# The column pass of an attention's preparation: columns copied into lines first, the projection in two strips of 64 rows

## The chip, the cores and the metric

The kernel runs on one core of a Trainium2 chip. A core has a matrix engine (TensorE, PE in the profile; its weight loads are listed apart as PEld), a vector engine (VectorE, DVE), a scalar engine (ScalarE, ACT), a general engine (GpSimd, POOL) and a queue engine (SyncE, SP) that here only issues transfers. They share an on-chip memory of 128 partitions (SBUF) and an accumulator memory with as many partitions in eight banks (PSUM), into which TensorE writes.

The metric is the time of one execution on the device in microseconds, the median of several runs. One more execution was recorded by the hardware profiler; its span runs from its first to its last instruction.

## What is computed

The input `x` is float32, (2, 128, 128, 128): two images of 128 channels, 128 rows h and 128 columns w. Four layers follow one another, each as `x = x + layer(group_norm(x))`: an attention along the columns, a recurrent convolution in four directions, a deformable convolution and a convolution in Hadamard form. Only the first is touched. In it every column w of an image is a sequence of 128 positions h:

```python
x = jnp.transpose(x, (0, 3, 1, 2))                 # (n, w, c, h)
x = x.reshape(NW, C, H)                            # 256 sequences
xg = x.reshape(NW, 8, C // 8, H)                   # 8 groups of 16 channels
wg = w_qkv.reshape(8, OUT * 2 // 8, C // 8)        # 32 outputs for each group
qkv = jnp.einsum('bgch,gdc->bgdh', xg, wg).reshape(NW, OUT * 2, H)
qkv = _bn(qkv, g_qkv, b_qkv, (0, 2), (1, OUT * 2, 1))
qkv = qkv.reshape(NW, GROUPS, GP * 2, H)
q, k, v = (qkv[:, :, :GP // 2], qkv[:, :, GP // 2:GP], qkv[:, :, GP:])
qr = jnp.einsum('bgci,cij->bgij', q, q_emb)
kr = jnp.einsum('bgci,cij->bgij', k, k_emb).swapaxes(2, 3)
qk = jnp.einsum('bgci,bgcj->bgij', q, k)
stacked = jnp.concatenate([qk, qr, kr], axis=1)
stacked = _bn(stacked, g_sim, b_sim, (0, 2, 3), (1, GROUPS * 3, 1, 1))
```

The projection `qkv` works within groups: the 32 outputs of a group (8 of q, 8 of k, 16 of v) depend on its own 16 channels alone. The batch norm over `qk` needs the mean and the mean square of all products q·k, and these follow from sums over the positions: for each sequence and group, the products of q with q and of k with k and the plain sums, an 8x8 block each and a column.

## The kernel before

`layer0_prepare` (line 92) keeps both images on chip as `xa[n]`, 128 channels on the partitions and (h, w) behind them, so that a row h is contiguous and the elements of a column lie 128 elements (512 bytes) apart. It has three stages.

The first (lines 116 to 320) loads the images, forms the channels' products for the norms, and folds group norm and batch norm into the projection. For the q and k outputs (k = 0) and the v outputs (k = 1), `psr` spreads scale and shift over all partitions, `rows[:, k]` (line 304, ScalarE) holds them, and `wz[n][:, k, :]` (line 307, VectorE) is the scaled weight matrix: 128 channels by 128 outputs, zero outside the groups' own blocks. Its q and k half has its columns ordered as q of all groups (64), then k of all groups (64).

The second stage is the column pass (lines 361 to 452), which the change is about. It takes 64 turns, each with four columns (`RT`) of one image:

- `sequences(i, vs)` (line 371) projects the four columns. For each column one matmul takes the column of `xa` as its weights (`lhsT`, 128 channels by 128 positions, 512 bytes between neighbours) and streams `wz[n]`, 256 outputs, so that the result has positions on the partitions and outputs along them. Two columns share one PSUM buffer `ps_zb` of one bank; there are four such buffers. VectorE adds the shifts (`along`, line 345) in two additions per pair: the q and k outputs go to `z`, one of two buffers `zb` with a column of ones after every 32 outputs, and the v outputs go to `vs`.
- `moments(z)` (line 400) multiplies the `z` of the turn before: 16 matmuls, each of a block of 32 outputs (four groups' q or k) against itself and the ones, in four column strips of the array. The results land in `ps_m`, where `[:, half, 0]` and `[:, half, 1]` are a q block and the k block of the same groups. ScalarE copies the q part to `gq`, VectorE multiplies it by the k part, GpSimd adds the product to `acc` (line 418).
- After every fourth turn the queue engine stores `vs`, 1 MB, to DRAM (line 432). `vs` has two buffers.

TensorE's order is written out by hand: the projection of turn i, then the moments of turn i - 1. `InOrder` (line 73) fixes this program order on TensorE, VectorE and ScalarE; instructions issued through `nc.vector` or `nc.gpsimd` directly may be moved by the scheduler. After the last turn the sums in `acc` become the scale of `qk` (`logit_scales`, through `psm`) and `onto`.

The third stage (lines 456 to 569) goes over the rows h in the same manner (`positions`, `ps_zt`, `zt`, then `pg`), and its `project` makes the q and k values that attention reads (`ps_q`, `sa`, `sb`). Both use only the q and k half, `wz[n][:, 0, :]`. Attention, `layer0_attention`, comes next; `lg<-qk` in the profile is its product of q and k, with the 8 channels of a group in strips of 32 array rows.

Most instructions are listed under line 81, the helper of `InOrder`, so the profile is read by the names of the tiles.

Of the kernel before, what the change touches and what calls it, by code (L numbers as in the profile page):

```python
# [7 lines left out]
F32 = mybir.dt.float32  # L8
I32 = mybir.dt.int32
AF = mybir.ActivationFunctionType  # L10
ALU = mybir.AluOpType
# [4 lines left out]
P = 128  # L16
N = 2
S = 128
RT = 4
# [72 lines left out]
def layer0_prepare(env, x, prm, mem, alphas):  # L92
# [4 lines left out]

    nc, tc = env.nc, env.tc  # L100
    HW = WC // 2
    with ExitStack() as ctx:
# [6 lines left out]
        strip, ones = late[:, 0:128], late[:, 128:256]  # L109
        gsim = kp.tile([P, NG, 3], F32, name="gsim", tag="gsim")  # L110
        rows = kp.tile([P, 2, 1 + N, P], F32, name="rows", tag="rows")
        wz = [kp.tile([P, 2, P], F32, name=f"wz{n}", tag=f"wz{n}") for n in range(N)]
        shift = kp.tile([P, N], F32, name="shift_qk", tag="shift_qk")
        eg = kp.tile([P, 9, S], F32, name="eg", tag="eg")

        with ExitStack() as early:
# [178 lines left out]
            for k in range(2):  # L295
                psr = pp.tile([P, 1 + N, P], F32, name="psr", tag="psr")
                for s in range(2):
                    dgs = wp.tile([P, 1 + N, P], F32, name="dgs", tag="dgs", bufs=2)
                    for c in range(1 + N):
                        nc.vector.tensor_scalar(  # L300
                            dgs[:, c, :], pick[:, k, s, :], cols[:, s, c : c + 1], None, ALU.mult
                        )
                    nc.tensor.matmul(psr, lhsT=ones, rhs=dgs, start=(s == 0), stop=(s == 1))
                nc.scalar.copy(rows[:, k], psr)
                lo = 256 + 128 * k
                for n in range(N):
                    nc.vector.scalar_tensor_tensor(
                        wz[n][:, k, :],
                        wt[:, lo : lo + P],
                        gs[:, n : n + 1],  # L310
                        rows[:, k, 0, :],
                        ALU.mult,
                        ALU.mult,
                    )
            psq = pp.tile([P, 1 + N], F32, name="psq", tag="ps_small")
            for s in range(2):
                nc.tensor.matmul(
# [27 lines left out]
        def along(n, k, shape):  # L345
            return (
                rows[:, k, 1 + n, :]
                .rearrange("p (b c) -> p b c", b=(4, NG)[k])
                .unsqueeze(1 if k == 0 else 2)
                .to_broadcast(shape)  # L350
            )
# [9 lines left out]
        with ExitStack() as part:  # L361
            sp = part.enter_context(tc.tile_pool(name="l0s", bufs=1))
            gp = part.enter_context(tc.tile_pool(name="l0g", bufs=2))
            pp = part.enter_context(tc.tile_pool(name="l0pm", bufs=2, space=PSUM))
            acc = sp.tile([P, 2, 33], F32, name="acc2", tag="acc2")
            nc.gpsimd.memset(acc, 0.0)
            zb = [sp.tile([P, RT, 4, 33], F32, name=f"zb{j}", tag=f"zb{j}") for j in range(2)]
            for t in zb:
                nc.gpsimd.memset(t[:, :, :, 32:33], 1.0)

            def sequences(i, vs):

                n, w = i // NT, i % NT * RT
                z = zb[i % 2]
                for hf in range(2):
                    ps = pp.tile([P, 2, 2, P], F32, name="ps_zb", tag="ps_zb", bufs=4)
                    for j in range(2):
                        pe.matmul(
                            ps[:, j],
                            lhsT=xa[n][:, :, w + 2 * hf + j],  # L380
                            rhs=wz[n],
                            start=True,
                            stop=True,
                        )
                    dve.tensor_tensor(
                        z[:, 2 * hf : 2 * hf + 2, :, 0:32],
                        ps[:, :, 0, :].rearrange("p w (b c) -> p w b c", b=4),
                        along(n, 0, [P, 2, 4, 32]),
                        ALU.add,
                    )  # L390
                    at = (w + 2 * hf) % HW
                    dve.tensor_tensor(
                        vs[:, :, at : at + 2, :],
                        ps[:, :, 1, :].rearrange("p w (g c) -> p g w c", g=NG),
                        along(n, 1, [P, NG, 2, 16]),
                        ALU.add,
                    )
                return z

            def moments(z):  # L400


                ps = pp.tile([P, 2, 2, 33], F32, name="ps_m", tag="ps_m")
                for half in range(2):
                    for b in range(2):
                        for s in range(4):
                            w, block = 2 * half + s // 2, 2 * b + s % 2
                            pe.matmul(
                                ps[32 * s : 32 * s + 32, half, b, :],
                                lhsT=z[:, w, block, 0:32],  # L410
                                rhs=z[:, w, block, :],
                                start=True,
                                stop=True,
                            )
                gq = gp.tile([P, 2, 33], F32, name="gq", tag="gq")
                act.copy(gq, ps[:, :, 0, :])
                dve.tensor_tensor(gq, gq, ps[:, :, 1, :], ALU.mult)
                nc.gpsimd.tensor_tensor(acc, acc, gq, ALU.add)

            z_last = None  # L420
            for i in range(N * NT + 1):
                if i < N * NT:
                    n, j = i // NT, i % NT
                    if j % 4 == 0:
                        vs = gp.tile([P, NG, HW, 16], F32, name="vs", tag="vs")
                    z = sequences(i, vs)
                if z_last is not None:
                    moments(z_last)
                if i < N * NT:
                    if j % 4 == 3:  # L430
# [25 lines left out]
        with ExitStack() as part:  # L456
# [9 lines left out]
            def positions(t):  # L466

                zs = []
                for n in range(N):
                    z = zt[2 * (t % 2) + n]  # L470
                    ps = pp.tile([P, RT, P], F32, name="ps_zt", tag="ps_zt")
                    for hh in range(RT):
                        pe.matmul(
                            ps[:, hh, :],
                            lhsT=xa[n][:, t * RT + hh, :],
                            rhs=wz[n][:, 0, :],
                            start=True,
                            stop=True,
                        )
                    dve.tensor_tensor(  # L480
                        z[:, :, :, 0:32],
                        ps.rearrange("p h (b c) -> p h b c", b=4),
                        along(n, 0, [P, RT, 4, 32]),
                        ALU.add,
                    )
                    zs.append(z)
                return zs
# [24 lines left out]
            def project(n, wc, b, sa, sb):  # L512
                ps = pp.tile([P, 16, WC], F32, name="ps_q", tag="ps_q")
                pe.matmul(
                    ps,
                    lhsT=wz[n][:, 0, :],
                    rhs=xa[n][:, b * 16 : (b + 1) * 16, wc * WC : (wc + 1) * WC],
                    start=True,
                    stop=True,
# [1631 lines left out]
```

## Time and profile before

| what | value |
|---|---|
| median of 3 runs | 5539.87 us (5536.61 to 5543.36) |
| the profiled execution, own time | 5539.68 us |
| its span | 5537.9 us |
| TensorE busy | 5230.7 us, 94% of the span |
| VectorE, ScalarE, GpSimd busy | 3687.8, 2604.6, 1546.4 us |
| mean granted TensorE clock | 0.973 |
| first projection of the column pass | 110.30 us |
| first projection of the row pass behind it | 271.40 us |

A group line of the profile gives line, engine, operation, output<-inputs, shapes and how often, then busy time and the mean of one in nanoseconds, then the idle time of the engine ahead of the group and what ended it. The groups of the column pass, from the first 500 us of the trace:

```profile
L81 PE MATMUL ps_zb<-wz,xa 128*128 128x256 f32 x512 | 138.1, 414 | 1.0 <-DVE wz L307 1.0
L81 PEld LDWEIGHTS ps_zb<-wz,xa 128*128 128x128 f32 x512 | 118.4, 303 | 5.7 <-DVE wz L307 2.1
L81 DVE TENSOR_TENSOR zb<-ps_zb,rows 128x256 f32<-128x256 f32 x128 | 54.4, 425 | 49.2 <-PE ps_zb L81 41.4
L81 DVE TENSOR_TENSOR vs<-ps_zb,rows 128x256 f32<-128x256 f32 x128 | 53.0, 414 | 0.0
L81 PE MATMUL ps_m<-zb 128*32 128x33 f32 x2048 | 29.5, 198 | 0.0
L81 DVE TENSOR_TENSOR gq<-gq,ps_m 128x66 f32<-128x66 f32 x64 | 14.3, 224 | 0.5 <-ACT gq L81 0.5
L81 ACT COPY gq<-ps_m 128x66 f32<-128x66 f32 x64 | 13.7, 215 | 145.9 <-PE ps_m L81 138.8 <-DVE zb L81 7.1
L418 POOL TENSOR_TENSOR acc<-acc,gq 128x66 f32<-128x66 f32 x64 | 20.8, 325 | 138.4 <-DVE gq L81 138.2
```

Each float32 matmul leaves two records on TensorE and two on its weight loads: 256 columns make 512 records. Matmuls are pipelined, so the mean of one record is longer than the distance between two.

### The profile page before, as it was taken

Reading aid. Unit: us, or ns where it says so; the run is one execution under the profiler, and the core shown is the slowest. Engines: PE = TensorE matmul, PEld = TensorE weight load, DVE = VectorE, ACT = ScalarE, POOL = GpSimd, SP = SyncE. Lnnn points to the kernel's source line nnn. Section 1 sums busy time; section 2 is a strip of 40 time slices with the busy share of each in tenths; the row PEclk is TensorE's granted clock in tenths of the full one; section 3 lists DMA queues with packets and bytes.
Section 4 is the critical chain, followed back from the end, with each engine's and each line's share of the span. In section 5 each row is a group of like instructions: output and inputs, shape, how many; then the busy total and the mean of one; then the engine's idle time right before and its main releaser. Section 6 shows DMA issues by size and latency. Waiting matters only on the chain. (4 is left out here: it accounts for less than half of the span.)

```text
span 5537.9 us, 171854 instructions
## 1 busy us (share of the span) xinstructions
PE 5230.7 (94%) x71931; PEld 4656.8 (84%) x71931; DVE 3687.8 (67%) x7132; ACT 2604.6 (47%) x8118; POOL 1546.4 (28%) x1169
## 2 busy tenths in 40 slices
PE   8997999999999908999999999999899999999999
PEld 6866888888888708999999999994799999999877
DVE  3635888888888866555555556663566666666798
ACT  1056989889888845552223330003233333333322
POOL 2114666666666632000000003330000000000376
PEclk8998999999999959999999999999999999999999
DMA  3353333333333389900000000104677767677111
GB/s 153 108 215 92 61 60 61 62 60 61 60 60 61 68 353 202 105 1 1 1 1 1 1 1 32 47 33 113 112 88 86 88 90 86 89 88 88 42 51 57
DMA packets 673354, 421.01 MB, mean 76 GB/s; under 512 B 325696, under 2 KB 630720, under 8 KB 660672
## 3 DMA queue, kind: packets, MB, share of 16 engines
q1 hardware_dynamic: 667406, 400.69, 39.1%
q8 instruction: 576, 9.44, 0.7%
q10 hardware_dynamic: 5170, 9.23, 0.5%
q14 instruction: 202, 1.65, 0.1%
HBM read 269.09 MB, written 157.45 MB: 77 GB/s over the span
## 5 line engine op out<-in xcount | busy, mean ns | idle before, releaser
L81 PE MATMUL pl<-ln,wl 128*128 128x128 f32 (+1 forms) x10160 | 1240.9, 276 | 9.7 <-DVE ln L81 8.2
L81 PEld LDWEIGHTS pl<-ln,wl 128*128 128x128 f32 x10160 | 1175.8, 190 | 23.0 <-issue 7.1
L81 ACT ACTIVATE e<-e,mx 128x128 f32<-128x128 f32 x2048 | 793.5, 395 | 0.8 <-DVE mx L81 0.8
L81 ACT COPY sm<-ps_s 128x432 f32<-128x432 f32 (+1 forms) x768 | 318.2, 487 | 834.2 <-PE ps_s L81 808.5
L81 POOL TENSOR_TENSOR e<-e,total 128x1024 f32<-128x1024 f32 x256 | 485.6, 1897 | 485.4 <-DVE total L81 473.5
L81 ACT COPY res<-ln 128x64 f32<-128x64 f32 (+1 forms) x1016 | 283.9, 304 | 701.2 <-DVE ln L81 701.2
L81 DVE COPY s<-ps_w 100x1152 f32<-100x1152 f32 x256 | 346.5, 1353 | 334.2 <-PE ps_w L81 334.2
L81 PE MATMUL ps_s<-s,xw 100*128 100x144 f32 x4096 | 546.5, 287 | 8.2 <-DMA xw<-px_d 8.2
L81 POOL TENSOR_TENSOR res<-ln,x1t 128x128 f32<-128x128 f32 x256 | 148.9, 582 | 1429.7 <-DVE ln L81 1429.7
L81 PE MATMUL po<-sm,wdef 128*128 128x256 f32 x2304 | 539.1, 379 | 0.0
L81 PE MATMUL pl<-ln,ws 128*128 128x128 f32 x4064 | 536.8, 273 | 0.0
L81 POOL COPY et<-et 128x1024 f32<-128x1024 f32 x256 | 517.1, 2020 | 33.7 <-DVE et L81 25.5
L81 PEld LDWEIGHTS ps_s<-s,xw 100*128 100x128 f32 x4096 | 518.2, 190 | 9.1 <-DMA xw<-px_d 8.6
L81 DVE TENSOR_TENSOR v<-pl,c 128x128 f32<-128x128 f32 x508 | 148.3, 292 | 539.4 <-PE pl L81 536.2
L81 PEld LDWEIGHTS pl<-ln,ws 128*128 128x128 f32 x4064 | 494.4, 190 | 0.0
L81 ACT ACTIVATE r<-gen,alphas 128x1536 f32<-128x1536 f32 x256 | 394.9, 1542 | 169.2 <-PE gen L81 141.5
L81 PEld LDWEIGHTS po<-sm,wdef 128*128 128x128 f32 x2304 | 419.8, 190 | 47.7
L81 POOL MEMSET col<- 128x10 f32 (+1 forms) x72 | 5.9, 121 | 1461.1 <-DVE res L81 1453.6
L81 ACT ACTIVATION_READ_ACCUMULATOR e<-e,mx 128x1 f32 x2048 | 397.2, 194 | 0.0
L81 DVE SCALAR_TENSOR_TENSOR ln<-v,res 128x128 f32<-128x128 f32 x1016 | 347.2, 342 | 48.6 <-POOL res L81 0.9
L81 PE MATMUL te<-cst_main,e 128*128 128x128 f32 x2048 | 338.4, 288 | 26.6 <-POOL e L81 20.1
L81 DVE COPY et<-te 128x512 f32<-128x512 f32 x512 | 348.4, 681 | 13.4 <-PE te L81 13.0
(244 smaller groups left out, 9144.7 us busy)
## 6 DMA issues: line engine op xcount, KB each, us to landing
xw<-px_d SPq DMA_DIRECT2D x1275, 80.0 KB
xa<-in_x SPq DMA_DIRECT2D x16, 1024.0 KB
v_d<-vs SPq DMA_DIRECT2D x16, 1024.0 KB
qb_d<-sb SPq DMA_DIRECT2D x16, 1024.0 KB
qa_d<-sa SPq DMA_DIRECT2D x8, 2048.0 KB
zz<-qb_d SPq DMA_DIRECT2D x1024, 16.0 KB
vt<-v_d SPq DMA_DIRECT2D x64, 256.0 KB
qk<-qa_d SPq DMA_DIRECT2D x256, 64.0 KB
```

The source lines that it names most:

```text
L81: return lambda *a, **k: self.tc.keep_in_program_order(issue(*a, **k))
```

## The change

- The four columns of a turn are first copied into lines. `columns(i)` lets ScalarE copy them from `xa` to `xc`, where each column is contiguous; `xc` has three buffers, and the copies run two turns ahead.
- The projection becomes two matmuls for each column: channels 0 to 63 (groups 0 to 3) and channels 64 to 127 (groups 4 to 7), each with 64 rows of the array and only the 128 outputs that belong to those groups. Their weights are `wzs[n]`, built by eight small VectorE instructions. `wz[n]` keeps the q and k half for the row pass.
- The result buffer `ps_zb` holds all four columns: two banks, one for each strip, two buffers instead of four. A matmul writes 128 outputs in runs of 16, so that the values of four columns lie side by side.
- VectorE makes three additions for a turn instead of four: two of 256 elements to `z` (q and k), one of 512 to `vs`. The shifts for `z` come from `along_qk`, which GpSimd reorders once.
- The order of blocks in `z` is now per strip, and `moments` picks its blocks accordingly. ScalarE copies all of `ps_m` (132 elements), and GpSimd makes the product that VectorE made, before its sum.

```diff
-        wz = [kp.tile([P, 2, P], F32, name=f"wz{n}", tag=f"wz{n}") for n in range(N)]
+        wz = [kp.tile([P, P], F32, name=f"wz{n}", tag=f"wz{n}") for n in range(N)]
+        wzs = [kp.tile([P, 2, 64], F32, name=f"wzs{n}", tag=f"wzs{n}") for n in range(N)]
+        along_qk = [kp.tile([P, 2, 64], F32, name=f"aqk{n}", tag=f"aqk{n}") for n in range(N)]
...
                 for n in range(N):
-                    nc.vector.scalar_tensor_tensor(
-                        wz[n][:, k, :],
-                        wt[:, lo : lo + P],
-                        gs[:, n : n + 1],
-                        rows[:, k, 0, :],
-                        ALU.mult,
-                        ALU.mult,
-                    )
+                    for s in range(2):
+                        half = slice(64 * s, 64 * s + 64)
+
+                        def own_groups(a):
+                            if k == 1:
+                                return a[half, half]
+                            return a[half].rearrange("p (b s c) -> p b s c", b=2, s=2)[:, :, s]
+
+                        to = wzs[n][half, 1 - k]
+                        nc.vector.scalar_tensor_tensor(
+                            to if k == 1 else to.rearrange("p (b c) -> p b c", b=2),
+                            own_groups(wt[:, lo : lo + P]),
+                            gs[half, n : n + 1],
+                            own_groups(rows[:, k, 0, :]),
+                            ALU.mult,
+                            ALU.mult,
+                        )
+            for n in range(N):
+                nc.vector.scalar_tensor_tensor(
+                    wz[n], wt[:, 256:384], gs[:, n : n + 1], rows[:, 0, 0, :], ALU.mult, ALU.mult
+                )
+                nc.gpsimd.tensor_copy(
+                    along_qk[n].rearrange("p s (b c) -> p s b c", b=2),
+                    rows[:, 0, 1 + n, :].rearrange("p (b s c) -> p s b c", b=2, s=2),
+                )
...
-            def sequences(i, vs):
+            def columns(i):
+
+                n, w = i // NT, i % NT * RT
+                xc = gp.tile([P, RT, S], F32, name="xc", tag="xc", bufs=3)
+                act.copy(xc, xa[n][:, :, w : w + RT].rearrange("p h w -> p w h"))
+                return xc
+
+            def sequences(i, vs, xc):
...
-                for hf in range(2):
-                    ps = pp.tile([P, 2, 2, P], F32, name="ps_zb", tag="ps_zb", bufs=4)
-                    for j in range(2):
+                ps = pp.tile([P, 2, 4, P], F32, name="ps_zb", tag="ps_zb")
+                for j in range(RT):
+                    for s in range(2):
+                        half = slice(64 * s, 64 * s + 64)
                         pe.matmul(
-                            ps[:, j],
-                            lhsT=xa[n][:, :, w + 2 * hf + j],
-                            rhs=wz[n],
+                            ps[:, s].rearrange("p g (k w c) -> p k g w c", k=2, w=RT)[:, :, :, j],
+                            lhsT=xc[half, j, :],
+                            rhs=wzs[n][half].rearrange("p k (g c) -> p k g c", g=4),
                             start=True,
                             stop=True,
                         )
+                def both(k):
+                    return ps[:, :, :, 64 * k : 64 * k + 64].rearrange(
+                        "p s g (w c) -> p (s g) w c", w=RT
+                    )
+
+                for e in range(2):
                     dve.tensor_tensor(
-                        z[:, 2 * hf : 2 * hf + 2, :, 0:32],
-                        ps[:, :, 0, :].rearrange("p w (b c) -> p w b c", b=4),
-                        along(n, 0, [P, 2, 4, 32]),
+                        z[:, :, :, 16 * e : 16 * e + 16].rearrange("p w j c -> p j w c"),
+                        both(1)[:, e::2],
+                        along_qk[n]
+                        .rearrange("p s (j c) -> p (s j) c", j=4)[:, e::2]
+                        .unsqueeze(2)
+                        .to_broadcast([P, 4, RT, 16]),
                         ALU.add,
                     )
-                    at = (w + 2 * hf) % HW
-                    dve.tensor_tensor(
-                        vs[:, :, at : at + 2, :],
-                        ps[:, :, 1, :].rearrange("p w (g c) -> p g w c", g=NG),
-                        along(n, 1, [P, NG, 2, 16]),
-                        ALU.add,
-                    )
+                at = w % HW
+                dve.tensor_tensor(
+                    vs[:, :, at : at + RT, :],
+                    both(0),
+                    rows[:, 1, 1 + n, :]
+                    .rearrange("p (g c) -> p g c", g=NG)
+                    .unsqueeze(2)
+                    .to_broadcast([P, NG, RT, 16]),
+                    ALU.add,
+                )
...
-                            w, block = 2 * half + s // 2, 2 * b + s % 2
+                            w, block = 2 * half + s // 2, 2 * (s % 2) + b
...
-                gq = gp.tile([P, 2, 33], F32, name="gq", tag="gq")
-                act.copy(gq, ps[:, :, 0, :])
-                dve.tensor_tensor(gq, gq, ps[:, :, 1, :], ALU.mult)
-                nc.gpsimd.tensor_tensor(acc, acc, gq, ALU.add)
+                gq = gp.tile([P, 2, 2, 33], F32, name="gq", tag="gq")
+                act.copy(gq, ps)
+                nc.gpsimd.tensor_tensor(gq[:, :, 0, :], gq[:, :, 0, :], gq[:, :, 1, :], ALU.mult)
+                nc.gpsimd.tensor_tensor(acc, acc, gq[:, :, 0, :], ALU.add)
 
             z_last = None
+            xcs = {i: columns(i) for i in range(2)}
             for i in range(N * NT + 1):
+                if i + 2 < N * NT:
+                    xcs[i + 2] = columns(i + 2)
...
-                    z = sequences(i, vs)
+                    z = sequences(i, vs, xcs.pop(i))
```

In the row pass `wz[n][:, 0, :]` becomes `wz[n]`, and the helper `along` is written out where it was used; nothing else changes there.

More of the change, by code (lines that the diff above doesn't have):

```diff
@@ L343, in logit_scales @@
             nc.vector.tensor_tensor(alphas[:, :, to], t3, gsim[:, :, to], ALU.mult)
[L345 to L350, printed above, removed]
-            )
         pe, dve, act = (InOrder(tc, e) for e in (nc.tensor, nc.vector, nc.scalar))
@@ L384, in sequences @@
                         )
-                    dve.tensor_tensor(
-                        z[:, 2 * hf : 2 * hf + 2, :, 0:32],
-                        ps[:, :, 0, :].rearrange("p w (b c) -> p w b c", b=4),
-                        along(n, 0, [P, 2, 4, 32]),
+                def both(k):
[3 more added lines that the diff above has]
+                for e in range(2):
+                    dve.tensor_tensor(
+                        z[:, :, :, 16 * e : 16 * e + 16].rearrange("p w j c -> p j w c"),
[4 more added lines that the diff above has]
+                        .to_broadcast([P, 4, RT, 16]),
                         ALU.add,
                     )
-                    at = (w + 2 * hf) % HW
-                    dve.tensor_tensor(
-                        vs[:, :, at : at + 2, :],
-                        ps[:, :, 1, :].rearrange("p w (g c) -> p g w c", g=NG),
-                        along(n, 1, [P, NG, 2, 16]),
-                        ALU.add,
-                    )
+                at = w % HW
[8 more added lines that the diff above has]
+                )
                 return z
@@ L475, in positions @@
                             lhsT=xa[n][:, t * RT + hh, :],
-                            rhs=wz[n][:, 0, :],
+                            rhs=wz[n],
                             start=True,
@@ L482, in positions @@
                         ps.rearrange("p h (b c) -> p h b c", b=4),
-                        along(n, 0, [P, RT, 4, 32]),
+                        rows[:, 0, 1 + n, :]
+                        .rearrange("p (b c) -> p b c", b=4)
+                        .unsqueeze(1)
+                        .to_broadcast([P, RT, 4, 32]),
                         ALU.add,
@@ L515, in project @@
                     ps,
-                    lhsT=wz[n][:, 0, :],
+                    lhsT=wz[n],
                     rhs=xa[n][:, b * 16 : (b + 1) * 16, wc * WC : (wc + 1) * WC],
```

## The prediction, before the result was known

> **What bounds the kernel now.** I read the page first for the span and busy shares (TensorE busy 94% of 5537.9 us), then the windows, which place the touched code: the column pass, the loop over `sequences` and `moments`, runs from about 110 to 271 us, 161 us of the whole. In it TensorE never rests:
>
> ```profile
> 150.00:200.00 50.00, 50.00 (x836) 44.36 (x834) 35.09 (x103) 4.29 (x20) 6.51 (x20) 1.00 0.32 107
> ```
>
> The columns are TensorE, weight load, VectorE, ScalarE, GpSimd busy us, then granted clock, DMA share, GB/s. TensorE is full at full clock, VectorE at 70%, ScalarE under a tenth. Waits of this stretch point the same way: every consumer waits for TensorE.
>
> ```profile
> ACT gq L81 <- PE ps_m L81: 132.0, 59, 2.5
> POOL acc L418 <- DVE gq L81: 125.5, 59, 2.5
> DVE zb L81 <- PE ps_zb L81: 36.0, 59, 0.6
> PEld ps_m L81 <- issue: 13.4, 59, 0.2
> ```
>
> Third, the timeline of one turn (four columns):
>
> ```profile
> 202.08 0.46 PE L81 MATMUL ps_m<-zb 128*32 128x33 f32 x32
> ...
> 202.47 1.83 PEld L81 LDWEIGHTS ps_zb<-wz,xa 128*128 128x128 f32 x8
> 202.47 2.13 PE L81 MATMUL ps_zb<-wz,xa 128*128 128x256 f32 x8
> ...
> 203.75 0.42 DVE L81 TENSOR_TENSOR zb<-ps_zb,rows 128x256 f32<-128x256 f32 x1 [0.61 <-PE ps_zb L81]
> 204.09 0.41 DVE L81 TENSOR_TENSOR vs<-ps_zb,rows 128x256 f32<-128x256 f32 x1
> 204.52 0.35 PEld L81 LDWEIGHTS ps_m<-zb 128*32 128x32 f32 x32 [0.23 <-issue]
> ```
>
> `moments` starts at 202.08, the projection at 202.47, the next `moments` at 204.52: 0.39 + 2.05. From the first `moments` (116.31) to the last but one (268.24) lie 62 turns: 2.45 us a turn. A float32 matmul leaves two records, so four columns make eight.
>
> **What the Trainium skill says.** "TensorEngine Tiling (Array Packing)", Key Properties and Gotcha 1: tiles in different rows run LdWeights and Matmul in parallel if they write different PSUM banks; changing the mode drains the array. The trace has this form already, attention's products of 8 rows in two row strips alternating between two banks:
>
> ```profile
> 704.72 1.16 PE L81 MATMUL lg<-qk 8*128 8x128 f32 x16
> ...
> 705.81 0.31 PEld L81 LDWEIGHTS te<-cst_main,e 128*128 128x128 f32 x3
> 705.81 0.44 PE L81 MATMUL te<-cst_main,e 128*128 128x128 f32 x2
> ```
>
> Sixteen records over 128 columns take 1.09 us from the first to the next mode's first (705.81 - 704.72), the drain included; the same width on the whole array takes 1.99 us for 16 (`ps_zt` starts at 279.65, the `pg` behind it at 281.64). So the overlap is real. "SBUF — State Buffer", the cacheline note under Door 1: stepping past 16 bytes at every access costs extra. The trace agrees: ScalarE's copy of a line, neighbours 8 bytes apart, against the same copy into a column:
>
> ```profile
> L81 ACT COPY res<-ln x64: 307/308/313, 2700.8 to 2798.7; 128x128 f32<-128x128 f32 x64
> L81 ACT COPY res<-ln x125: 407/413/420, 2999.8 to 3198.8; 128x128 f32<-128x128 f32 x125
> ```
>
> +105 ns over 128 elements, 0.82 ns each. "PSUM — Partial Sum Buffer", Specifications, says that non-contiguous patterns slow matmuls; no run here shows an output in pieces of 16.
>
> **The change, part by part.**
>
> *TensorE projection.* Removed per turn: four matmuls of 128 rows by 256 columns, 2.05 us with their strided weight load. Added: eight matmuls of 64 rows by 128 columns, 16 records in alternating strips, each strip with its own bank. The nearest row is `lg<-qk`, the same count, width, alternation and banks; only the rows (8 of a strip, here 64) and the output (pieces of 16) differ. I take 1.09 us. Below: 0.97, the stretch of the sixteen `lg<-qk` weight loads, if the drain hid. Above: no overlap at all, 1.99 as `ps_zt`. For scattered output I take nothing extra, because each piece is 64 contiguous bytes; if it doubled the passes the group would cost 1.9. `moments` keeps its 16 matmuls and two mode switches: 0.39. TensorE's turn is 1.48 us.
>
> *ScalarE.* Added: 64 copies of 128x512 from columns 512 bytes apart. Contiguous, 512 elements cost 586 ns (`xt`); with 0.82 x 512 = 420 ns for the stride, 1.0 us. The bounds are 0.6 (no penalty) and 1.1 (the 128x1024 copy `u`, written with a stride, takes 2.21 us). `gq` grows from 66 to 132 elements: 215 + 66 x 0.83 (from `rows`, 384 elements in 478 ns) = 270 ns. Together 1.27, and consecutive ACTIVATEs overlap by about 0.1 each (`sa` lasts 0.78, its successor starts 0.66 after it), so about 1.2 with waits, 0.3 below TensorE's turn. Behind each waiting `gq` the next column copy is queued, but it is for a turn two ahead, so its lateness is covered by about one turn.
>
> *VectorE.* Removed: four adds of 256 elements and the 224 ns product. Added: two adds of 256 (0.425 each) and one of 512 (0.69, as `zt`). Neighbours start 0.34 apart (203.75, 204.09) for 256; two `zt` take 1.29, so 0.60 for 512. Sum 0.34 + 0.34 + 0.60 = 1.28, against 1.48. Pieces of 16 instead of 32 in the output: below, no difference; above, 0.6 an add, 1.8 in all. I take no difference. PSUM goes from four one-bank buffers to two of two banks: the projection after next needs the last add, 1.41 us after its matmuls end, while TensorE returns to that buffer after 0.39 + 1.09 + 0.39 = 1.87. There is 0.46 to spare.
>
> *GpSimd.* Gains the product, about the price of its sum (325 ns), plus a hand-over of some 0.1 each: 0.85 of a 1.48 turn, and nobody but the end waits for it. Two copies to `along_qk` fit while TensorE makes the second `psr`.
>
> *SP's queue.* The same 16 stores of 1 MB, now every 5.9 us instead of 9.8. The last one issued at 269.12 let `zt` go at 274.50, 5.4 us later; a `vs` buffer is wanted again after 5 x 1.48 - 0.6 = 6.8. Hidden with 1.4 us to spare; a landing above 6.8 would put its excess into every fourth turn.
>
> *Head.* Before, `rows` ends at 109.86 and the first projection starts at 110.30. Now the first column copy stands behind `rows` on ScalarE (1.0 us), and its buffer may also have to wait for the four small weight products on VectorE (0.17 each, about 0.7, interpolated between 161 ns for 2 and 347 ns for 128 elements). That is +0.6 to +1.5; I take +1.1. The two full `wz` products run under the second `psr`.
>
> *End.* `zt` waits for the last store, which waits for the last `vs` add: 0.8 us behind the last projection before, 1.41 now, so +0.6. The added GpSimd product (+0.3 on the path to `psm`) lies under that wait.
>
> **Sum**: 64 x (2.45 - 1.48) = 62.1, less 1.1, less 0.6 = 60.4 us. Everything later waits on data, not on the clock: the next pass starts with `zt`, attention with its loads, so the gain should pass through whole. The profiled execution took 5539.68 (span 5537.9 plus 1.8 around it), 0.2 below the median of 5539.87, so both give 5479.
>
> **Rivals.**
> - *TensorE sets the turn, 1.42 to 1.55* (forecast, chance 0.74): 5475 to 5484. For it: `lg<-qk`.
> - *ScalarE becomes the bound* (0.10): its copy costs 1.5 to 2.0 us because reads a row apart are dearer than writes were. At 1.8 the turn is 1.8 + 0.27 - 0.1 (overlap less waits) = 1.97 and the time 5539.7 - 30.7 + 1.7 = 5511. Against it: two measured strides give 0.8 to 1.1 ns per element.
> - *VectorE or the PSUM pieces set it* (0.08): a turn of 1.65 to 1.9, 5490 to 5506. For it: the page on PSUM; against it: runs of 64 bytes.
> - *The strips don't overlap, so the change doesn't do what it says* (0.05): a turn of 1.99 + 0.39 = 2.38 gains 4.5, head and end give 1.7 back: 5537. Against it: the 1.09 us above.
> - *Slower* (0.03): one mechanism, ScalarE's strided read, decides from a copy of 2.28 us, 4.5 ns per element (turn 2.45). At 3 us the turn is 3.17 and the time 5539.7 + 46 + 1.7 = 5587. No ScalarE copy of more than 200 elements in this trace costs over 2.2 ns per element.
>
> **How the numbers follow.** The likeliest case gives 5479. The range reaches from 5470 (projection at its low end, a turn of 1.36, and a head of 0.6: 69.8 - 1.2 = 68.6) to 5512 (ScalarE bound at 1.8 us a copy); it leaves out half of the second case and all of the last two. A measurement of this kernel can tell about 0.2%, 11 us, from no change: faster takes the first three cases, 0.92; same the fourth, 0.05; slower the last, 0.03.
>
> **What would show it.** Right: the column pass lasts about 100 us; `ps_zb` records come in pairs, 0.11 to 0.14 us from pair to pair, and `moments` starts 1.1 us after the projection; ScalarE's copy `xc` is near 1.0 us and its `gq` waits for TensorE; VectorE idles a little before each first add. Wrong: TensorE idle behind `xc` (ScalarE bound) or behind the adds (VectorE or buffers), matmul records of equal spacing above 100 ns (no overlap), or a `vs` add that waits for a store. The prediction fails most readily on ScalarE's copy, whose read from columns no row of this trace shows.

## The result, and the profile after

The changed kernel takes 5504.9 us (median of four runs, 5498.7 to 5506.5) against 5538.2 for the kernel before on the same chip: a ratio of 0.9938, with a 95% interval of 0.9926 to 0.995. That is 33 us less by the medians and 34 by the ratio, whose interval reaches from 28 to 41. The forecast was 60. The profiled execution of the changed kernel took 5498.68 us, the lowest of its four, so 41 less than the profiled one before.

The page of the changed kernel gives a span of 5496.8 us and this busy time of the engines:

```profile
PE 5176.2 (94%) x72443; PEld 4608.0 (84%) x72443; DVE 3663.1 (67%) x7010; ACT 2672.4 (49%) x8182; POOL 1565.9 (28%) x1235
```

TensorE is busy for 54 us less than before and the span is 41 us shorter: some of what the projection gave back has become idle time. Where, the marks of the stages say. The first projection of the column pass starts at 112.65 us (before 110.30), the first `ps_zt` of the row pass at 235.44 (before 271.40). Of the 2.35 us at the head, 0.33 lie ahead of the second `rows`, which the change does not touch and which starts between 108.66 and 111.84 us in the runs of this study; the change itself made 2.0. The pass shrank from 161.1 to 122.8 us, by 38.3. At the row pass the lead is 36.0; it drifts up to 41 by the end in this pair of executions, more than the medians show.

Now one turn of the new pass, where nothing disturbs it; the columns are start, duration, engine and operation, and in brackets the idle time ahead:

```profile
221.00 0.46 PE L81 MATMUL ps_m<-zb 128*32 128x33 f32 x32
...
221.40 1.16 PE L81 MATMUL ps_zb<-wzs,xc 64*128 64x128 f32 x16
221.62 0.27 ACT L81 COPY gq<-ps_m 128x132 f32<-128x132 f32 x1 [0.20 <-PE ps_m L81]
221.78 1.12 ACT L81 COPY xc<-xa 128x512 f32<-128x512 f32 x1
221.79 0.68 DVE L81 TENSOR_TENSOR vs<-ps_zb,rows 128x512 f32<-128x512 f32 x1
...
222.49 0.46 PE L81 MATMUL ps_m<-zb 128*32 128x33 f32 x32
222.60 0.76 DVE L81 TENSOR_TENSOR zb<-ps_zb,aqk 128x256 f32<-128x256 f32 x2
```

From `moments` to `moments` it is 222.49 - 221.00 = 1.49 us, made of 0.40 and 1.09. The forecast's turn is there to the hundredth. ScalarE waits for TensorE before `gq`, and the column copy behind it ends before the next `gq`. VectorE is done with `vs` at 222.47 and starts its next addition at 222.60, just behind the end of the projection (221.40 + 1.16 = 222.56). But 62 such turns would take 91.9 us, and from the first `moments` to the last but one they take 113.5. The pass is not slow, it is interrupted. TensorE's waits for "issue" from 112 to 240 us (time in total, how often, the longest):

```profile
PE ps_m L81 <- issue: 11.1, 8, 2.1
PE ps_zb L81 <- issue: 3.5, 3, 2.3
```

In eleven stretches, 14.6 us together, TensorE waits for "issue": for nothing that another engine or a data transfer releases. Before, the stretch of 150 to 200 us had no idle time at all. One of the eleven, with what follows it:

```profile
137.33 0.41 PE L81 MATMUL ps_m<-zb 128*32 128x33 f32 x25
139.81 0.27 PE L81 MATMUL ps_m<-zb 128*32 128x33 f32 x7 [2.07 <-issue]
140.00 1.16 PE L81 MATMUL ps_zb<-wzs,xc 64*128 64x128 f32 x16
141.10 0.65 PE L81 MATMUL ps_m<-zb 128*32 128x33 f32 x32
141.68 2.08 PE L81 MATMUL ps_zb<-wzs,xc 64*128 64x128 f32 x16
143.69 0.67 PE L81 MATMUL ps_m<-zb 128*32 128x33 f32 x32
144.29 1.28 PE L81 MATMUL ps_zb<-wzs,xc 64*128 64x128 f32 x16
```

TensorE stops in the middle of `moments`, after 25 of its 32 records. No buffer and no wait lies between the 25th and the 26th: all read one `z` and write one `ps_m`. And shortly after the restart the matmuls run at half speed for some 3 us (2.08 us for a group of 1.16); the granted clock in the trace is 0.5 from 141.2 to 144.6 us. The windows around the stop give the busy time of TensorE, its weight loads, VectorE, ScalarE and GpSimd, the granted clock, the DMA share and GB/s:

```profile
133.40:137.00 3.60, 3.06 (x96) 2.73 (x98) 2.39 (x6) 1.83 (x4) 0.81 (x3) 1.00 0.88 291
137.50:139.80 2.30, 0.24 (x25) 0.16 (x17) 1.30 (x3) 0.25 (x1) 0.00 (x0) 1.00 0.00 0
```

Just ahead of the stop the DMA engines are full, with a store of `vs`; during it there is no traffic. What moved is in the DMA queues (packets, MB, share of the engines), first from 133 to 137.2 us, then from 137.2 to 139.9:

```profile
q1 hardware_dynamic: 1034, 1.04, 74.9%
...
q8 instruction: 1, 0.02, 2.2%
```

Queue 8 brings instructions, in blocks of 16 KB. From 112 to 230 us it brings 24; 64 turns of 96 TensorE instructions (48 matmul records and as many weight loads) are about 256 to a block (6144 / 24), by this estimate 64 bytes each. At 1.48 us a turn, a block lasts 256 / 96 x 1.48 = 3.95 us. While the 1 MB of `vs` pours out for about 3.5 us, no block of queue 8 starts; the next one comes at 137.5, right behind it, and TensorE resumes 2.3 us later. So it is with nine of the eleven stops: in the packets of the trace the block starts within 0.03 us of the end of a store. The other two, of 0.30 and 0.18 us, are the shortest. Behind every one of the eleven, TensorE goes on 1.3 to 1.6 us after the block's packet has ended. In the kernel before the order is the same (122.9 to 126.5 us, then 126.5 to 128.5):

```profile
q1 hardware_dynamic: 1038, 1.05, 86.1%
...
q8 instruction: 1, 0.02, 3.5%
```

but there a turn has 80 instructions in 2.45 us, a block lasts 7.8 us, and TensorE does not feel it. So the theory after the result, called F below: the faster turn uses up its instructions in about the time that a store blocks their arrival. Its rival R: 96 instructions in 1.48 us are more than can be brought in any case, and the store has no part in it. A second rival, M: store and compute contend for the on-chip memory. This stretch speaks against M: during the store the projections keep their 1.16 us (those at 134.75 and 136.24), and the stop lies behind the store, when nothing moves.

### The profile page after: what moved, and what is told of

It reads as the page before. It is cut to its first block, busy times and chain, and to the rows that moved or that the text cites. A ratio compares the mean times of both kernels' runs of the same rounds, so it can differ in the third digit from the quotient of the medians.

```text
span 5496.8 us, 172767 instructions
## 1 busy us (share of the span) xinstructions
PE 5176.2 (94%) x72443; PEld 4608.0 (84%) x72443; DVE 3663.1 (67%) x7010; ACT 2672.4 (49%) x8182; POOL 1565.9 (28%) x1235
## 5 line engine op out<-in xcount | busy, mean ns | idle before, releaser
L81 PEld LDWEIGHTS po<-sm,wdef 128*128 128x128 f32 x2304 | 419.8, 190 | 47.6
L81 PE MATMUL gen<-zz,toep 32*128 32x128 f32 x8192 | 334.1, 288 | 23.2 <-DMA zz<-qb_d 15.2
```

The source lines that it names most:

```text
L81: return lambda *a, **k: self.tc.keep_in_program_order(issue(*a, **k))
```

## Experiments

**The change once more** (`a0_change_again`), to see whether the stops have fixed places.

> The changed kernel once more, as the base of this set. Theory F (TensorE runs out of instructions, because the fetch of the next 16 KB waits behind a whole 1 MB store of vs): median near 5505, several idle stretches of 1 to 2.3 us on TensorE in the column pass with no releaser, at other places than in the first trace where the order of fetch and store falls out otherwise, so times that scatter by some 8 us. Rival R (the fetch itself is too slow for 65 instructions per us, stores or not): the same stretches at about the same places.

Measured: 5506.42 us (5500.57 to 5510.76), ratio 0.9932 (0.9916 to 0.9949). TensorE's waits for "issue" from 112 to 240 us are 13.6 us ahead of records of `ps_m` and 2.7 ahead of `ps_zb`. The pass begins 1.1 us later here; apart from that most stops stand where they stood. Two of them, first in the trace shown above, then in this one:

```profile
162.99 0.26 PE L81 MATMUL ps_m<-zb 128*32 128x33 f32 x4 [1.87 <-issue]
168.96 0.39 PE L81 MATMUL ps_m<-zb 128*32 128x33 f32 x23 [1.45 <-issue]
```

```profile
164.30 0.26 PE L81 MATMUL ps_m<-zb 128*32 128x33 f32 x4 [1.86 <-issue]
170.28 0.39 PE L81 MATMUL ps_m<-zb 128*32 128x33 f32 x23 [1.46 <-issue]
```

Ten of the eleven stops recur at the same matmul record, and there are two more. F had expected other places and R about the same ones, so in this respect the run went against F as it was put on record. But the places hold a stronger sign. Counted in matmul records from the start of the pass, the stops of the first trace come behind record 556, 681, 1308, 1433, 1684 and so on, always a whole multiple of 125 to 126 apart. With as many weight loads these are about 251 instructions, close to the 256 estimated for a block; the profile does not list every instruction. All 57 waits for "issue" in the column pass, of this kernel and of the runs below, lie on these places, and each ends 1.2 to 1.6 us after a block of queue 8 has arrived. A stop is the end of one instruction block and the wait for the next; which ends become stops, and how long they are, differs from run to run.

**No store** (`e1_no_store`). The stores of `vs` are left out; attention loads rows of the input in their place, in the same amount.

```diff
-                    if j % 4 == 3:
-                        lo = j // 4 % 2 * HW
-                        nc.sync.dma_start(
-                            out=mem["v"][:, n, j // 8, :, lo : lo + HW, :].rearrange(
-                                "g h w c -> h g (w c)"
-                            ),
-                            in_=vs.rearrange("p g w c -> p g (w c)"),
-                        )
...
-            sync.dma_start(out=u.v, in_=mem["v"][u.g, u.n, u.wc])
+            sync.dma_start(
+                out=u.v.rearrange("p w c -> p (w c)"),
+                in_=prm["x"][u.n, :, 4 * u.g : 4 * u.g + 4, :].rearrange("p h w -> p (h w)"),
+            )
```

> Leaves the 16 stores of vs out; attention loads rows of the input in their place, in the same amount. Theory F: every turn 1.48 us, no idle stretch without a releaser in the column pass, first ps_zt at 112.7 + 64 x 1.48 + 4 = 212 instead of 235.4, and a time of about 5505 - 22 = 5483. Rival R: the idle stretches stay, 5505 less at most 1 for the end.

Measured: 5480.55 us (5477.16 to 5483.4), ratio 0.9887 (0.987 to 0.9903). The window of 120 to 210 us, and TensorE's waits in it:

```profile
120.00:210.00 90.00, 89.66 (x2888) 79.43 (x2879) 81.12 (x180) 76.30 (x119) 37.08 (x120) 1.00 0.02 5
```

```profile
PE ps_zb L81 <- issue: 0.3, 1, 0.3
```

For comparison the changed kernel in the same window:

```profile
120.00:210.00 90.00, 77.47 (x2284) 67.92 (x2273) 64.34 (x144) 60.58 (x97) 29.11 (x95) 0.94 0.43 143
```

TensorE is busy 89.66 of 90 us instead of 77.47, at full clock instead of 0.94, with the same instructions: R falls, since the fetch keeps up when nothing is stored. From the first projection to the row pass it takes 101.4 us (114.12 to 215.49) instead of 122.8. F had expected 5483. The whole time is within 2 us of the forecast's 5479: the forecast's turn describes the kernel without its stores. That the whole sum agrees so closely is in part luck, since head and end were sized wrongly (below).

**Stores of half the size, and of twice** (`e2_half_stores`, `e3_double_stores`): 32 stores of 0.5 MB from four half buffers, or 8 stores of 2 MB.

```diff
-                    if j % 4 == 0:
-                        vs = gp.tile([P, NG, HW, 16], F32, name="vs", tag="vs")
+                    if j % 2 == 0:
+                        vs = gp.tile([P, NG, 8, 16], F32, name="vs", tag="vs", bufs=4)
...
-                    if j % 4 == 3:
-                        lo = j // 4 % 2 * HW
+                    if j % 2 == 1:
+                        lo = j // 2 % 4 * 8
```

```diff
-                    if j % 4 == 0:
-                        vs = gp.tile([P, NG, HW, 16], F32, name="vs", tag="vs")
+                    if j % 8 == 0:
+                        vs = gp.tile([P, NG, 32, 16], F32, name="vs", tag="vs")
...
-                    if j % 4 == 3:
+                    if j % 8 == 7:
```

> The same data in 32 stores of 0.5 MB, one after every second turn, four vs buffers of half the size. Theory F: a fetch waits at most for some 1.6 us, less than the 3.9 us that a block of 16 KB lasts, so nearly all idle stretches go and the time is about 5483 to 5488. Rival R: 5505. If runs of 512 bytes make the stores slower, bursts touch each other and the gain shrinks.

> The same data in 8 stores of 2 MB, one after every eighth turn. Theory F: a burst lasts 6.2 us, longer than a block of instructions, so each of the eight costs 2 to 5 us and the column pass is longer than with 16 stores: idle stretches of 16 to 40 us in sum instead of 14.6, single ones up to 5 us, and 5505 to 5530. Rival R: 5505.

Measured: half 5492.39 us (5489.16 to 5493.19), ratio 0.9908 (0.9892 to 0.9925); double 5509.93 (5503.62 to 5517.5), ratio 0.9944 (0.9927 to 0.996). TensorE's waits for "issue" from 120 to 210 us, with half stores:

```profile
PE ps_zb L81 <- issue: 5.0, 7, 1.6
PE ps_m L81 <- issue: 3.7, 5, 1.5
```

and with double stores:

```profile
PE ps_zb L81 <- issue: 6.7, 2, 3.9
PE ps_m L81 <- issue: 6.5, 3, 3.1
```

The longest stop goes with the size of the store, 1.6, then 2.3 in the change itself, then 3.9 us, while the number of stops goes the other way (12, 8 and 5 in this window). That is the direction F gives, and double stores came out at the low end of what it expected. With half stores F was wrong: nearly all stops were to go, because a fetch would wait at most some 1.6 us, less than a block lasts, and the time was to be 5483 to 5488; 8.7 us of idle time remained in this window. As recorded, F is too simple in two respects. The block must come and TensorE goes on only 2.3 us after its start, so a burst and these 2.3 us have to fit into the time that a block lasts; with the figures above, an estimate of 3.5 + 2.3 = 5.8 us against 3.95 in the change and 7.8 before. And the bursts touch, which the expectation had named as a danger: half stores write runs of 512 bytes instead of 1 KB, for the same 16.8 MB the share of the store queue in the DMA engines' time, 112 to 236 us, rises from 40.3% to 47.6%, and the packets show unbroken bursts (no gap over 0.05 us) of 1.9 to 5.2 us, half of them over 2.7, against a median of 3.6 in the change. So this comparison is not of the burst's length alone.

**Copies alone, strips alone** (`e4_copy_only`, from the kernel before: ScalarE copies the columns into lines, the projection keeps 128 rows and 256 outputs; `e5_strips_only`, from the changed kernel: two strips, but the weights are taken from `xa` with its stride and nothing is copied).

```diff
+                if i + 2 < N * NT:
+                    xcs[i + 2] = columns(i + 2)
...
-                            lhsT=xa[n][:, :, w + 2 * hf + j],
+                            lhsT=xc[:, 2 * hf + j, :],
```

```diff
-                            lhsT=xc[half, j, :],
+                            lhsT=xa[n][half, :, w + j],
...
-                if i + 2 < N * NT:
-                    xcs[i + 2] = columns(i + 2)
```

> The kernel before with one part of the change: ScalarE puts the four columns in line, the projection stays at 128 rows by 256 outputs with the contiguous columns as weights. If the gain comes from the strips: TensorE's turn falls only from 2.45 to about 2.3 (the first two matmuls of a turn 0.1 us closer, the other records stay near 0.22 apart because they stream 256 columns), 5530 to 5540. If it comes from contiguous weights: a turn well below 2, below 5510. 80 TensorE instructions in 2.3 us last longer than a store's burst, so no idle stretch without a releaser.

> The change without ScalarE's copies: the two strips take their weights straight from the image, 512 bytes between neighbours. If the copies are needed: loading 128 strided weights, some 0.2 us each, sets the distance between pairs, a turn of about 2.2 and 5525 or so. If the other strip's matmuls hide the strided loads: 1.48 plus the idle stretches and, with no copy ahead of the first projection, about 1 us less than the change, 5503.

Measured: copies alone 5533.15 us (20 runs), ratio 0.9986 (0.9979 to 0.9992); strips alone 5533.95 us, ratio 0.9985 (0.9979 to 0.9992). Each gives about 8 us, together they give 34, so neither part explains the gain by itself. Copies alone came out as expected; strips alone, with a turn of 2.35 us, are slower than both of the recorded cases (2.2 a turn and 5525, or 1.48 and 5503). The projection of a turn with the copies alone, and the `moments` behind it:

```profile
202.35 1.99 PE L81 MATMUL ps_zb<-wz,xc 128*128 128x256 f32 x8
204.28 0.46 PE L81 MATMUL ps_m<-zb 128*32 128x33 f32 x32
```

The contiguous weight load is quick now, but eight records of 256 columns still take 1.93 us. A turn of the strips alone:

```profile
201.08 0.46 PE L81 MATMUL ps_m<-zb 128*32 128x33 f32 x32
201.47 2.02 PE L81 MATMUL ps_zb<-wzs,xa 64*128 64x128 f32 x16
203.43 0.46 PE L81 MATMUL ps_m<-zb 128*32 128x33 f32 x32
```

Half as many columns stream by in each strip, and the 16 records still take 1.96 us: the load of a strided weight lasts 310 ns (its median) against 188 for the line, longer than the 272 ns of a matmul record in the change. Copy and strip lift two limits that lie at nearly the same height.

For F this run says more. It has the same 96 TensorE instructions a turn and the same sixteen stores of 1 MB, and no stop at all:

```profile
120.00:210.00 90.00, 90.00 (x1836) 83.83 (x1834) 51.92 (x115) 10.20 (x38) 23.93 (x78) 1.00 0.36 119
```

A block lasts 256 / 96 x 2.35 = 6.3 us here, longer than a burst and the fetch behind it (5.8). It is the pace of the instructions that makes the store hurt, not the strips nor the number of instructions. ScalarE's copies are missing here too; but they run on without the stores and with the paced ones, where the stops go, so it is not they that stop TensorE.

**Paced stores** (`e6_paced`). Each store of `vs` goes out in four quarters of 256 KB, one a turn; ahead of the second to the fourth stands a store of 64 bytes from the turn's own `vs`, which holds the queue until that turn is done. `vs` gets a third buffer.

```diff
+            sync, parts = InOrder(tc, nc.sync), []
+
+            def store():
+
+                to, at, q = parts.pop(0)
+                sync.dma_start(
+                    out=to[2 * q : 2 * q + 2].rearrange("g h w c -> h g (w c)"),
+                    in_=at[:, 2 * q : 2 * q + 2].rearrange("p g w c -> p g (w c)"),
+                )
...
+                    if parts:
+                        at = j % 4 * RT
+                        sync.dma_start(out=mem["pace"][i : i + 1], in_=vs[0:1, 0, at, :])
+                        store()
                     if j % 4 == 3:
...
+                        parts += [(to, vs, q) for q in range(4)]
+                        store()
```

> The change with each 1 MB store cut into four of two groups, one after each turn: ahead of the second to fourth the store queue writes 64 bytes of the turn's own vs to a scratch row, which makes it wait for that turn; three vs buffers. Theory F: a burst is 0.8 us with runs of 1 KB, so a fetch waits at most that long, the idle stretches go but for some tenths, and the time is that without stores, 5481 to 5485. If even short bursts hold the fetch up for longer than they last, 5490 as with the half stores.

Measured: 5487.04 us (5485.77 to 5488.8), ratio 0.9902 (0.9885 to 0.9918). Window and waits:

```profile
120.00:210.00 90.00, 87.46 (x2743) 76.91 (x2740) 76.85 (x171) 72.99 (x115) 35.04 (x114) 1.00 0.49 162
```

```profile
PE ps_zb L81 <- issue: 1.4, 3, 0.5
PE ps_m L81 <- issue: 1.0, 3, 0.5
```

More bytes per microsecond than in the change (162 GB/s against 143), and a fifth of the idle time, at full clock. This too speaks against M: contention would grow with the traffic. What the instructions need is a gap in it. The third buffer is not what helps, since no addition waited for a store in the change. The time is 2 us above the 5481 to 5485 expected; the stops that remain, of up to 0.65 us in the whole pass, stand at ends of blocks as before. The quarters do not all stand alone: half of the unbroken bursts last 1.0 us or less, the longest 3.1. From the first projection to the row pass it takes 107.2 us (114.79 to 222.0), 15.6 less than in the change and 5.8 more than without stores.

**Paced stores, and the first copies early** (`e7_paced_early`). The first two column copies are issued before `psr`, into buffers of their own, so that the first projection no longer waits for them.

```diff
+            xcs = {i: columns(i) for i in range(2)}
             for k in range(2):
...
             z_last = None
-            xcs = {i: columns(i) for i in range(2)}
```

> As e6, and the first two column copies stand ahead of psr on ScalarE in buffers of their own, so that the first projection waits for its weight product alone: 0.65 us behind rows instead of 2.5. 1.5 to 2 us less than e6, 5479 to 5484. If ScalarE's early copies delay rows, nothing or a loss of up to 2 us.

Measured: 5486.06 us (5484.58 to 5486.48), ratio 0.99 (0.9884 to 0.9917). The head of this kernel:

```profile
102.45 2.02 ACT L81 COPY xc<-xa 128x512 f32<-128x512 f32 x2
...
112.37 1.96 PE L81 MATMUL ps_zb<-wzs,xc 64*128 64x128 f32 x13 [0.88 <-DVE wzs L331]
```

The first projection now waits for the small products alone. From the end of `rows` to it 0.4 us pass (112.00, the end of its copy of 0.48 that starts at 111.52, to 112.37), where in the change and in the paced kernel a copy made it 2.5: 2.1 are gained at this place. The early copies delay nothing that counts: ScalarE is idle for 3.6 us between them and the next `rows`, and from the last activation ahead of the copies (`r`) to the first `rows` it takes 5.8 us with them (102.23 to 108.03) as without (102.56 to 108.35 in the paced kernel). The medians differ by 1 us (1.5 to 2 and a time of 5479 to 5484 were expected), and the spreads of both kernels leave too little of it to call it shown for the whole time. As a version it is the best of the study, about 55 us below the kernel before.

## Why the prediction was right and wrong

*The turn*: right. The forecast had 1.48 us for TensorE's turn; the trace shows 1.48 to 1.49 wherever no store disturbs it. The pairing of strips holds with 64 rows as with the 8 of attention's product, and writing the output in runs of 16 costs nothing: 1.09 us for the group, as for attention's product. The slowdown for non-contiguous output that the prediction quoted and set aside does not show with these pieces of 64 bytes.

*ScalarE, VectorE, PSUM*: right. The groups:

```profile
L81 ACT COPY xc<-xa x64: 1054/1112/1135, 111.5 to 226.2; 128x512 f32<-128x512 f32 x64
...
L81 DVE TENSOR_TENSOR zb<-ps_zb,aqk x128: 411/420/426, 114.8 to 230.4; 128x256 f32<-128x256 f32 x128
```

The column copy takes 1.11 us, the upper bound given (1.0 was taken); `gq` takes 0.27 as forecast; the additions have their old prices, 0.42 and 0.68, in spite of the pieces. None of the rivals that put the bound on ScalarE or VectorE took place. The measured time does lie in the band of the VectorE rival (5490 to 5506), but by chance: the undisturbed turn is 1.48, not 1.65 to 1.9 us, and TensorE waits for no addition of the pass. That the time lies inside the stated range, 5470 to 5512, is luck as well: its far end was put there for a slow column copy, and what was lost has a cause that no rival named.

*The step that failed* is the one on SP's queue. It asked only when a `vs` buffer comes free again, found 1.4 us to spare, and called the stores hidden. They are, as buffers: no addition waits for a store. But the stores are also traffic, in bursts of 3.5 us that now come every 5.9 us, and on the same DMA engines arrive TensorE's instructions. The prediction counted what the change does to each engine's work and never to the rate at which it eats instructions: from 80 in 2.45 us to 96 in 1.48, twice as fast. Its size: 62 turns took 113.5 us instead of 91.9, so 21.6 us. Of that the view of waits shows 13.3 as idle time (14.6 less 1.3 behind the last projection). The slower clock after three stops adds some 4.3: the turns behind each take about 1.4 us more than at full clock (for the one shown, three turns from 140.00 to 145.89 are 5.89 instead of 4.45). About 3 more come from a stop being longer than its idle time, by 0.2 to 0.5 us each, probably because the ends of matmuls are modelled: at the one shown, the next projection starts at 140.00 instead of 137.72, 2.3 late for an idle time of 2.07. The last 1.1 lie in four turns without a stop and were not explained; 1.7 of excess are left without stores too. That the loss hangs on the stores is shown by leaving them out; that bursts and not bytes cause it, by pacing them; that it takes the fast turn as well, by the strips alone. That the missing thing is the block of queue 8 rests on the places of the stops, which are ends of blocks, on the arrival of a block ahead of each restart, and on these three; no run changed the fetch itself. When a block is asked for, and why TensorE goes on only 2.3 us after its start, stays open.

The sign could have been seen before the change. In attention, from 427 to 1900 us, the kernel before has such stops on the many short matmuls of `po`, all 23 of them ending 1.2 to 1.9 us after a block of queue 8 has arrived:

```profile
PE po L81 <- issue: 16.8, 23, 1.3
```

*The head* was sized at 1.1 us and took 2.0. The stretch in the changed kernel:

```profile
109.71 0.48 ACT L308 COPY rows<-psr 128x384 f32<-128x384 f32 x1 [3.02 <-PE psr L307]
110.22 1.17 DVE L320 SCALAR_TENSOR_TENSOR wzs<-wt,gs_l,rows 64x64 f32<-64x64 f32 x4 [1.58 <-ACT rows L308]
111.54 2.99 ACT L81 COPY xc<-xa 128x512 f32<-128x512 f32 x3 [1.36 <-DVE wzs L320]
112.65 1.65 PE L81 MATMUL ps_zb<-wzs,xc 64*128 64x128 f32 x12 [2.98 <-ACT xc L81]
```

The text named both costs, the copy and its wait for the small products, but the sum took little more than the first. They stand one behind the other: four products of 0.29 (0.17 was interpolated), then the copy of 1.1. *The end* was put at +0.6; from the last projection's end to `ps_zt` it takes 3.2 us before (268.24 to 271.40), 4.1 with the stores left out and 5.5 in the changed kernel, where another stop of 1.26 lies in it: +2.4. The path was another one than forecast, too. The first `zt` had waited 0.6 us for the last store and no longer does; VectorE's sum `tot` waits for GpSimd instead, 0.5 us before, 1.2 without stores and 2.7 in the change. GpSimd's added product, which the text had put under the wait for the store, stands on that path.

With these sizes, 60.4 less 21.6 (turns), 0.9 (head), 1.8 (end) and the 0.3 by which this run was late ahead of the head makes 35.8, against the 36.0 at the start of the row pass. What makes the medians differ by a little less, and this pair by more at the end, is not settled; both lie inside the spread of the runs.

## What to carry to other kernels

When a change makes a loop of many short matmuls faster, work out how long one block of instructions lasts in the new loop, and compare it with the longest unbroken burst of data in the same stretch plus the time from a block's start to the restart, here 2.3 us; a wait for "issue" in the middle of a group of equal matmuls, just behind a burst, is its sign. What helped here was not less traffic but traffic with gaps: four stores of 256 KB, one in each turn, brought back most of what one store of 1 MB took. And two limits of equal height, here the strided weight load and the width of the stream, have to be lifted together, or neither edit shows its worth.

## What the runs showed that was not expected

- TensorE stops only where one instruction block (16 KB) ends and the next has not come: 57 stops in seven traces, all at whole multiples of 125 to 126 matmul records from one another. In the changed kernel nine of eleven ended with a block that started when a store of 1 MB ended, and TensorE went on some 2.3 us after that start. Some blocks did start inside a store (one at 216.7 us, in a store that moved from 212.8 to 217.1), so a store delays a block without always holding it to the end. The loss was 14.6 us of idle time, up to 2.3 us a stop, and up to 3.9 with stores of 2 MB.
- After three of the stops, of about 2 us each, TensorE slowed down soon after the restart: a group of 1.16 us took up to 2.08, for some 3 us, and about 1.4 us were lost each time. Without such stops (no store, paced stores) the granted clock from 120 to 210 us stayed at 1.00; in the change it was 0.94. It is not every such stop: after one of 1.87 us (at 162.99) the turns kept their 1.48, and with half stores, stops of up to 1.6 us, the clock stayed at 1.00.
- A strided weight load (512 bytes between neighbours) holds a pair of row strips to 0.25 us, as long as one record of 256 columns on the whole array; with contiguous weights the pair takes 0.14.
